# Attention values of 512 queries in every fourth slot, with the softmax sums applied after the product

## The chip, the cores and the metric

The kernel runs on one core of a Trainium2 chip. The metric is the device time of one execution in microseconds. The names of the engines are those of the profile: PE (TensorE, with PEld for its weight loads), DVE (VectorE), ACT (ScalarE), POOL (GpSimd) and SP (SyncE, which issues nearly all transfers of the kernel before).

## The reference

All data are float32. A graph-attention layer comes first, and then a transformer block whose attention is the part that matters here. It has four batches of 1024 rows, 16 heads of 64 columns, and nothing is masked:

```
qkv  = modulate(layernorm(x)) @ W_qkv          # x: 4 x 1024 x 512
attn = softmax(q @ k.T * 64**-0.5)             # per batch and head: 1024 x 1024
out  = attn @ v                                # 4 x 1024 x (16 heads x 64)
x    = x + g_msa * (out @ W_out + b_out)
x    = x + g_mlp * (gelu(modulate(layernorm(x)) @ W1 + b1) @ W2 + b2)
```

## The kernel before

The graph layer runs up to about 410 us of the span. The attention stage follows, to about 2226 us, and then the MLP.

The attention stage is cut into `NS` = 256 **slots**: four batches, eight pairs of heads (`gp`), eight tiles `t` of 128 queries. Slot `s` makes the scores of its 128 queries against all 1024 keys for both heads of the pair (`scores`, L1156: four matmuls in the program, eight records in the profile), into two PSUM tiles `psc` of two banks each, of which there are two, so that a slot's scores wait until both exponentials of the slot before have read them. VectorE takes the two maxima (`largest`, L1167), ScalarE makes the two exponentials with their sums (`weights`, L1173). `scaled` (L1178 to L1182) inverts each sum on VectorE and multiplies the 128x1024 weights by it, for head 0 on ScalarE (L1180), for head 1 on GpSimd (L1182). `turn` (L1191) transposes the weights on VectorE in blocks of 32x32 into `wd`; it is called for the slot before, head 0 at the beginning of a slot, head 1 after the two maxima.

Two successive slots make a **unit** `k` of 256 queries. When the second of them is transposed, eight copies of 256 KB (four for each head, L1195) issued by SP carry `wd` into `wT`, where the keys stand on the partitions. `wd` has three buffers, each for one head of one unit; `wT` has two, each for a whole unit. `attend` (L1064) multiplies a unit's `wT` with the values: 16 matmuls of 256 columns in the program, 32 records in the profile. ScalarE copies the product from PSUM to `oT` (L1076).

The rest of the work is laid between as fill: the projections of q, k and v for later heads in a form with seven products instead of eight (`seven`, L533, with VectorE's corrections in L547 and L551), the output projection in the same form (`out_step`, L1139), whose products VectorE adds to the rows `xr` (L1148), and sums of weights on GpSimd (L504 to L512). A planner places the fill: every item has a first and a last slot, a weight in units of TensorE's time, and a place within the slot. It looks for the slots in which the sum of the squares of the loads is small, with a price on two value products in one slot. `LAG` = 4 sets the distance from a unit's first slot to its `attend`:

```
lo = at + QT * k + LAG
add(lo, lo + (lo < NS - 8), 2, 1, attend, b, gp, k)
```

Within an engine the instructions run in the order in which the program gives them. Tiles are rotated within their pool: a tile that takes over a buffer waits for the last use of the one before it, on whichever engine that is.

```
wd[j] = ap_.tile([P, 4 * KC, QT, U], F32, name="wd", tag="wd", bufs=3)
wT[b, gp, k] = ap_.tile([P, 2, 4, KC, QT * U], F32, name="wT", tag="wT", bufs=2)
```

Of the kernel before, what the change touches and what calls it, by code (L numbers as in the profile page):

```python
# [41 lines left out]
def cond_block_kernel(  # L42
# [898 lines left out]
    with ExitStack() as actx:  # L941
# [9 lines left out]
        NB = S // QB  # L951
        wout, gate = {}, {}
        vt, oT, xr, wn, wd, wT = {}, {}, {}, {}, {}, {}

        turns = []

# [98 lines left out]
        def attend(b, gp, k, a=0, z=KC):  # L1055

            if a == 0:
                pav[0] = ps.tile([P, F], F32, name="pav", tag="pav")[:, :QB]
            po = pav[0]
            g, p = divmod(gp, 2)  # L1060
            w = wT[b, gp, k]
            for m in range(a, z):
                for j in range(2):
                    nc.tensor.matmul(  # L1064
                        po[j * D : (j + 1) * D, :],
                        lhsT=vt[b, g][:, m, p * P + j * D : p * P + (j + 1) * D],
                        rhs=w[:, j, :, m, :],
                        start=(m == 0),
                        stop=(m == KC - 1),
                    )  # L1070
# [53 lines left out]
        def out_step(b, g, u, k):  # L1124
            which, fresh, (i, j) = PU[k]
            if fresh:
                pu[0] = ps.tile([P, F], F32, name="pu", tag="pu")
            if which in SUM_A:
                a = osum[b, g][:, SUM_A[which] * HB : (SUM_A[which] + 1) * HB]
            else:  # L1130
                h, f = {0: (0, 0), 1: (0, 1), 3: (1, 1), 6: (1, 0)}[which]
                a = oT[b, 2 * g + f, u][:, h * QB : (h + 1) * QB]
            if which in SUM_B:
                r = wsum[b, g][:, SUM_B[which] * HB : (SUM_B[which] + 1) * HB]
            else:
                f, h = {0: (0, 0), 1: (1, 0), 2: (1, 1), 6: (0, 1)}[which]
                r = wout[b, g][:, f, h * HB : (h + 1) * HB]
            for q in range(2):
                nc.tensor.matmul(  # L1139
                    pu[0][:, q * HB : (q + 1) * HB],  # L1140
                    lhsT=a[:, q * P : (q + 1) * P],
                    rhs=r,
                    start=(bool(fresh) and q == 0),
                    stop=True,
                    skip_group_check=True,
                )
            o = xr[b, 2 * u + i][:, :, j * HB : (j + 1) * HB]
            nc.vector.tensor_tensor(o, pu[0].rearrange("p (r f) -> p r f", r=2), o, ALU.add)  # L1148


        def scores(b, gp, t):
# [15 lines left out]
            nc.vector.tensor_reduce(mx, sc, axis=AX.X, op=ALU.max, negate=True)  # L1167
            return mx

        def weights(sc, mx):  # L1170
            w = ap_.tile([P, S], F32, name="w", tag="w", bufs=4)
            sm = ap_.tile([P, 1], F32, name="sm", tag="sm", bufs=4)
            nc.scalar.activation(w, sc, AF.Exp, bias=mx, accum_out=sm)  # L1173
            return w, sm

        def scaled(j, w, sm):

            nc.vector.reciprocal(sm, sm)  # L1178
            if j == 0:
                nc.scalar.mul(w, w, sm)  # L1180
            else:
                nc.gpsimd.tensor_scalar(w, w, sm, None, ALU.mult)  # L1182

        def turn(b, gp, t, j):

# [54 lines left out]
        for b in range(B):  # L1240
# [252 lines left out]

        row_sum(0, 2)
        emit(-3, 0)
        before = None
        for s in range(NS + 1):
            if before is not None:
                turn(*before[0], 0)
            while later:  # L1500
                later.pop(0)()
            if s < NS:
                b, r = divmod(s, NP * NT)
                gp, t = divmod(r, NT)
                sc = scores(b, gp, t)
                mx = [largest(sc[j]) for j in range(2)]
                early(s)
                ws = [weights(sc[j], mx[j]) for j in range(2)]
                now = ((b, gp, t), ws)
                scaled(0, *ws[0])  # L1510
            if before is not None:
                turn(*before[0], 1)
            before = None
            if s < NS:
                scaled(1, *ws[1])
                for j in range(2):
                    wn[(*now[0], j)] = ws[j][0]
                before = now
            if s < NS:
                emit(s, s + 1)  # L1520
        sc_banks = halves()
        late = []
        second = with_four(
# [199 lines left out]
```

## Time and profile before

| | |
|---|---|
| time, median of 3 runs | 3037.48 us (3035.5 to 3040.55) |
| span of the profiled execution | 3034.2 us; the median lies 3.3 us above it |
| busy: PE, DVE, ACT, POOL | 99%, 66%, 47%, 44% |
| copies wT<-wd | 1024 of 256 KB |
| TensorE's granted clock | 1.00 in every stretch looked at |

The profile is of one execution. A row of the page's groups gives the line, the engine, the operation, what it writes and reads, how often, the busy time and the mean length of one, and then the engine's idle time just before and who ended it. In the chain and in the timeline the first number is the start in us, the second the length. SPq stands for SP's queue of transfers. TensorE runs each float32 matmul as two records.

### The profile page before, as it was taken

To read this page: it belongs to the slowest core of one execution; us is meant where nothing else is said; L and a number is where in the kernel's file an instruction comes from. 1 tells how busy PE (TensorE), PEld (TensorE's weight loads), DVE (VectorE), ACT (ScalarE), POOL (GpSimd) and SP (SyncE) were. 2 spreads that over 40 slices of the span, in tenths; PEclk is the share of its full clock that TensorE was granted. 3 is DMA by queue.
4 is the path that set the end of the run, shared out by engine and by line. 5 is a ranking of instruction groups with operands and counts; after the bars stand their busy time and mean duration, and the time that the engine had idled before them with its cause. 6 is when DMAs were issued, how large, how long until landed. Compare 5 with 4: busy or idle time off the path is not lost.

```text
span 3034.2 us, 41780 instructions
## 1 busy us (share of the span) xinstructions
PE 2999.3 (99%) x15317; PEld 1980.2 (65%) x15317; DVE 1999.6 (66%) x2836; ACT 1432.0 (47%) x2368; POOL 1339.4 (44%) x922
## 2 busy tenths in 40 slices
PE   9999999999999999999999999999999999999999
PEld 6666655555555555555555555555568888888888
DVE  3888867777878877878787878877863222222322
ACT  3344456555755565755555755556641221112211
POOL 1444456555656655656655656655721110111010
PEclk9999999999999999999999999999999999999999
DMA  6433357777868777768777868766871010101110
GB/s 201 140 118 121 117 129 180 162 171 179 192 157 210 181 168 179 192 155 211 187 159 180 191 159 205 189 162 164 203 196 63 14 49 28 49 21 35 35 42 15
DMA packets 282695, 417.90 MB, mean 138 GB/s; under 512 B 28968, under 2 KB 101092, under 8 KB 282492
## 3 DMA queue, kind: packets, MB, share of 16 engines
q1 hardware_dynamic: 282256, 415.03, 53.8%
q8 instruction: 123, 2.02, 0.3%
q14 instruction: 80, 0.66, 0.1%
q10 hardware_dynamic: 236, 0.20, 0.0%
HBM read 120.93 MB, written 25.76 MB: 48 GB/s over the span
## 4 chain that ended last, share of the span: by engine, by line
PE 83%; DVE 7%; ACT 3%; POOL 3%; issue 2%; DMA 2%; SPq 1%; POOLq 0%; DVEq 0%; ACTq 0%
PE q L533 19%; PE psc L1156 15%; PE pav L1064 13%; PE pu L1139 6%; PE mbd L533 5%; PE mbu L533 5%; PE mad L533 4%; PE mau L533 3%; PE mcd L533 2%; PE mdd L533 2%; PE mdu L533 2%; PE mcu L533 2%; DVE mx L1167 1%; ACT w L1173 1%; POOL t L742 1%
## 5 line engine op out<-in xcount | busy, mean ns | idle before, releaser
L1182 POOL TENSOR_SCALAR w<-w,sm 128x1024 f32<-128x1024 f32 x256 | 728.6, 2846 | 701.5 <-DVE sm L1178 686.4
L1173 ACT ACTIVATE w<-psc,mx 128x1024 f32<-128x1024 f32 x512 | 570.7, 1115 | 642.6 <-DVE mx L1167 641.6
L1191 DVE STREAM_TRANSPOSE wd<-w 128x1024 f32<-128x1024 f32 x512 | 632.2, 1235 | 109.3 <-ACT w L1180 96.0
L1167 DVE TENSOR_REDUCE mx<-psc 128x1 f32<-128x1024 f32 x512 | 599.2, 1211 | 80.2 <-PE psc L1156 77.0
L1156 PE MATMUL psc<-kT,qT 64*128 64x512 f32 x2048 | 526.9, 615 | 3.1 <-ACT kT L1024 1.4
L1064 PE MATMUL pav<-wT,v 128*64 128x256 f32 x4096 | 482.1, 383 | 1.2 <-DMA wT<-wd 0.6
L1064 PEld LDWEIGHTS pav<-wT,v 128*64 128x64 f32 x4096 | 296.1, 137 | 224.0 <-issue 86.0
L1156 PEld LDWEIGHTS psc<-kT,qT 64*128 64x128 f32 x2048 | 201.6, 186 | 220.5 <-issue 151.2
L1180 ACT ACTIVATE w<-w,sm 128x1024 f32<-128x1024 f32 x256 | 291.0, 1137 | 0.0
L512 POOL TENSOR_TENSOR tx<-hT 128x512 f32<-128x512 f32 x8 | 10.3, 1288 | 596.5 <-ACT hT L448 596.5
L1148 DVE TENSOR_TENSOR xr<-pu,xr 128x512 f32<-128x512 f32 x210 | 143.5, 683 | 78.9 <-PE pu L1139 78.7
L533 PE MATMUL q<-hT,wqk 128*128 128x512 f32 (+1 forms) x396 | 181.2, 581 | 1.0 <-DVE q L547 1.0
L555 ACT COPY mbu<-mau 128x512 f32<-128x512 f32 x30 | 17.1, 570 | 276.5 <-PE mau L533 276.5
L719 PE MATMUL pa<-kp,sfT 128*128 128x320 f32 x512 | 143.5, 433 | 1.4 <-ACT sfT L694 1.4
L533 PEld LDWEIGHTS q<-hT,wqk 128*128 128x128 f32 x396 | 74.7, 190 | 80.9 <-issue 78.2
L533 PE MATMUL q<-tx,ex 128*128 128x512 f32 (+1 forms) x264 | 123.5, 591 | 1.8 <-POOL tx L618 1.3
L719 PEld LDWEIGHTS pa<-kp,sfT 128*128 128x128 f32 x512 | 94.8, 190 | 38.2 <-ACT sfT L694 1.9
L679 PE MATMUL pf<-wx,xT 128*128 128x512 f32 x256 | 116.0, 596 | 0.0
L533 PE MATMUL mad<-w,hs 128*128 128x256 f32 x512 | 113.1, 379 | 0.0
L533 PEld LDWEIGHTS mad<-w,hs 128*128 128x128 f32 x512 | 97.3, 190 | 13.2
L1139 PE MATMUL pu<-wout,oT 128*128 128x256 f32 x360 | 98.4, 396 | 4.2 <-DVE xr L1148 3.7
L1139 PEld LDWEIGHTS pu<-wout,oT 128*128 128x128 f32 x360 | 62.6, 189 | 59.3 <-issue 31.6
(309 smaller groups left out, 4590.7 us busy)
## 6 DMA issues: line engine op xcount, KB each, us to landing
wT<-wd SPq DMA_DIRECT2D x1024, 256.0 KB
wqk<-in_w_qkv SPq DMA_DIRECT2D x64, 256.0 KB
xT<-in_xt SPq DMA_DIRECT2D x32, 256.0 KB
xs<-in_x SPq DMA_DIRECT2D x32, 256.0 KB
x1d<-xs SPq DMA_DIRECT2D x32, 256.0 KB
xl<-x1d SPq DMA_DIRECT2D x32, 256.0 KB
wv<-in_w_qkv SPq DMA_DIRECT2D x32, 256.0 KB
xr<-x1d SPq DMA_DIRECT2D x32, 256.0 KB
```

What stands on the lines that cost most here:

```text
L533: nc.tensor.matmul(t[:, q * width : (q + 1) * width], lhsT=lhs(which, q, k), rhs=rhs(which, q, k), start=(fresh and q == 0 and k == 0), st ...
L679: nc.tensor.matmul(pfs[i], lhsT=xT[i][:, c, :], rhs=wx[:, c, :], start=False, stop=(c == FC - 1), skip_group_check=True,)
L719: nc.tensor.matmul(pas[i][:, n, :HF], lhsT=sfT2[i][:, c, :], rhs=kp[:, b, c, n * HF : (n + 1) * HF], start=False, stop=(c == FC - 1), skip ...
L1064: nc.tensor.matmul(po[j * D : (j + 1) * D, :], lhsT=vt[b, g][:, m, p * P + j * D : p * P + (j + 1) * D], rhs=w[:, j, :, m, :], start=(m == 0),
L1139: nc.tensor.matmul(pu[0][:, q * HB : (q + 1) * HB], lhsT=a[:, q * P : (q + 1) * P], rhs=r, start=(bool(fresh) and q == 0), stop=True, skip ...
L1148: nc.vector.tensor_tensor(o, pu[0].rearrange("p (r f) -> p r f", r=2), o, ALU.add)
L1156: nc.tensor.matmul(sc[j][:, n * F : (n + 1) * F], lhsT=qT[b, gp][q, t * P : (t + 1) * P], rhs=kT[b, gp][q, n * F : (n + 1) * F], start=Tru ...
L1167: nc.vector.tensor_reduce(mx, sc, axis=AX.X, op=ALU.max, negate=True)
L1173: nc.scalar.activation(w, sc, AF.Exp, bias=mx, accum_out=sm)
L1180: nc.scalar.mul(w, w, sm)
L1182: nc.gpsimd.tensor_scalar(w, w, sm, None, ALU.mult)
L1191: nc.vector.transpose(wd[j][:, :, at, :], wn.pop((b, gp, t, j)).rearrange("p (m k) -> p m k", k=U))
```

## The change

The weights are no longer scaled. The exponentials leave their sums in one small tile per unit (`sm`, 128x4, in `weights`); when a unit's second slot is done, `scales_out` inverts the four columns on VectorE, and a slot later a DMA issued by ScalarE writes them to a small DRAM tile `scd`; two slots after the unit `scales_in` reads them back with two more DMAs of ScalarE's, spread over 64 partitions for each head (`rB`). VectorE multiplies the value product in PSUM with `rB` on its way to `oT`, in place of ScalarE's copy.

`turn` is called for the slot's own weights, both heads after the exponentials, instead of for those of the slot before. The weights `w` have two buffers instead of four.

Where a pair of heads is not among the last two, `attend_two` replaces two calls of `attend`: the value products of units 2u and 2u+1 follow each other into one PSUM bank, as one item of weight 4, with the first slot at the second unit's place.

The products of the output projection leave PSUM by a copy of ScalarE's into `po` (two buffers), and GpSimd adds them to `xr`.

```diff
+    scd = [tc.dram_tile([4, P], F32, name=f"scd{i}") for i in range(4)]
...
-            nc.scalar.copy(
+            nc.vector.tensor_tensor(
                 oT[b, gp, u][:, i * QB : (i + 1) * QB].rearrange("p (t u q) -> p u t q", t=QT, u=4),
                 po.rearrange("p (u t q) -> p u t q", t=QT, u=4),
+                rB.pop((b, gp, k)).rearrange("p (t u q) -> p u t q", t=QT, u=4),
+                ALU.mult,
             )
+        def attend_two(b, gp, u):
+            po = ps.tile([P, F], F32, name="pav", tag="pav")
+            g, p = divmod(gp, 2)
+            for k in (2 * u, 2 * u + 1):
+                w = wT[b, gp, k]
+                for m in range(KC):
+                    for j in range(2):
+                        nc.tensor.matmul(
+                            po[j * D : (j + 1) * D, k % 2 * QB : (k % 2 + 1) * QB],
+                            lhsT=vt[b, g][:, m, p * P + j * D : p * P + (j + 1) * D],
+                            rhs=w[:, j, :, m, :],
...
+            t = op_.tile([P, F], F32, name="oT", tag="oT", bufs=6)
+            oT[b, gp, u] = t
+            for k in range(2):
+                cols = slice(k * QB, (k + 1) * QB)
+                nc.vector.tensor_tensor(
...
-            nc.vector.tensor_tensor(o, pu[0].rearrange("p (r f) -> p r f", r=2), o, ALU.add)
+            t = ap_.tile([P, F], F32, name="po", tag="po", bufs=2)
+            nc.scalar.copy(t, pu[0])
+            nc.gpsimd.tensor_tensor(o, t.rearrange("p (r f) -> p r f", r=2), o, ALU.add)
...
-            w = ap_.tile([P, S], F32, name="w", tag="w", bufs=4)
-            sm = ap_.tile([P, 1], F32, name="sm", tag="sm", bufs=4)
-            nc.scalar.activation(w, sc, AF.Exp, bias=mx, accum_out=sm)
+            w = ap_.tile([P, S], F32, name="w", tag="w", bufs=2)
+            if (b, gp, k) not in esum:
+                esum[b, gp, k] = ap_.tile([P, 2 * QT], F32, name="sm", tag="sm", bufs=2)
+            c = j * QT + at
+            nc.scalar.activation(w, sc, AF.Exp, bias=mx, accum_out=esum[b, gp, k][:, c : c + 1])
...
+        def scales_out(b, gp, k):
+            sm = esum.pop((b, gp, k))
             nc.vector.reciprocal(sm, sm)
-            if j == 0:
-                nc.scalar.mul(w, w, sm)
-            else:
-                nc.gpsimd.tensor_scalar(w, w, sm, None, ALU.mult)
+            spot[0] += 1
+            scales[b, gp, k] = scd[spot[0] % len(scd)]
+            return lambda: nc.scalar.dma_start(scales[b, gp, k].rearrange("c p -> p c"), sm)
+        def scales_in(b, gp, k):
...
+                nc.scalar.dma_start(
+                    rB[b, gp, k][j * D : (j + 1) * D, :],
+                    row(rows[j * QT : (j + 1) * QT, :].rearrange("t q -> (t q)")).broadcast_to([D, QB]),
+                )
...
-                for k in range(NB):
+                if at < NS - 2 * NT:
+                    for u in range(NB // 2):
+                        lo = at + QT * (2 * u + 1) + LAG
+                        add(lo, lo + 1, 4, 1, attend_two, b, gp, u)
+                for k in range(NB if at >= NS - 2 * NT else 0):
                     lo = at + QT * k + LAG
...
+            sc = scores(b, gp, t)
+            mx = [largest(sc[j]) for j in range(2)]
+            early(s)
+            for j in range(2):
+                weights(b, gp, t, j, sc[j], mx[j])
+            for j in range(2):
+                turn(b, gp, t, j)
+            while coming and coming[0][0] <= s:
+                coming.pop(0)[1]()
+            if t % QT == QT - 1:
+                key = b, gp, t // QT
+                coming.append((s + 1, scales_out(*key)))
+                coming.append((s + 2, lambda key=key: scales_in(*key)))
+            emit(s, s + 1)
```

In the changed file the maxima are L1199, the exponentials L1208, the reciprocals L1214, the DMAs of the sums L1217 and L1224, the transposes L1236, the copies L1240, the double value product L1093 with the multiplications L1104, and the output products' copy and addition L1179 and L1180. Slot numbers below count within a pair of heads, from its first slot; unit k has the slots 2k and 2k+1, and where the text speaks of slot X, it is 4u+6, the first in which the double product of units 2u and 2u+1 may stand.

More of the change, by code (lines that the diff above doesn't have):

```diff
@@ L953, in cond_block_kernel @@
         vt, oT, xr, wn, wd, wT = {}, {}, {}, {}, {}, {}
+        esum, scales, rB, spot = {}, {}, {}, [0]
         turns = []
@@ L1075, in attend @@
                 oT[b, gp, u] = op_.tile([P, F], F32, name="oT", tag="oT", bufs=6)
-            nc.scalar.copy(
+            nc.vector.tensor_tensor(
                 oT[b, gp, u][:, i * QB : (i + 1) * QB].rearrange("p (t u q) -> p u t q", t=QT, u=4),
                 po.rearrange("p (u t q) -> p u t q", t=QT, u=4),
-            )
+                rB.pop((b, gp, k)).rearrange("p (t u q) -> p u t q", t=QT, u=4),
+                ALU.mult,
+            )
+        def attend_two(b, gp, u):
[9 more added lines that the diff above has]
+                            rhs=w[:, j, :, m, :],
+                            start=(m == 0),
+                            stop=(m == KC - 1),
+                        )
[4 more added lines that the diff above has]
+                nc.vector.tensor_tensor(
+                    t[:, cols].rearrange("p (t u q) -> p u t q", t=QT, u=4),
+                    po[:, cols].rearrange("p (u t q) -> p u t q", t=QT, u=4),
+                    rB.pop((b, gp, 2 * u + k)).rearrange("p (t u q) -> p u t q", t=QT, u=4),
+                    ALU.mult,
+                )
         def project(b, g, n):
@@ L1168, in largest, with weights @@
             return mx
-        def weights(sc, mx):
-            w = ap_.tile([P, S], F32, name="w", tag="w", bufs=4)
-            sm = ap_.tile([P, 1], F32, name="sm", tag="sm", bufs=4)
[L1173 to L1178, printed above, removed]
-            if j == 0:
-                nc.scalar.mul(w, w, sm)
-            else:
-                nc.gpsimd.tensor_scalar(w, w, sm, None, ALU.mult)
+        def weights(b, gp, t, j, sc, mx):
+            k, at = divmod(t, QT)
+            w = ap_.tile([P, S], F32, name="w", tag="w", bufs=2)
[3 more added lines that the diff above has]
+            nc.scalar.activation(w, sc, AF.Exp, bias=mx, accum_out=esum[b, gp, k][:, c : c + 1])
+            wn[b, gp, t, j] = w
+        def scales_out(b, gp, k):
+            sm = esum.pop((b, gp, k))
+            nc.vector.reciprocal(sm, sm)
+            spot[0] += 1
+            scales[b, gp, k] = scd[spot[0] % len(scd)]
+            return lambda: nc.scalar.dma_start(scales[b, gp, k].rearrange("c p -> p c"), sm)
+        def scales_in(b, gp, k):
+            rows = scales.pop((b, gp, k))
+            rB[b, gp, k] = ap_.tile([P, QB], F32, name="rB", tag="rB", bufs=4)
+            for j in range(2):
+                nc.scalar.dma_start(
+                    rB[b, gp, k][j * D : (j + 1) * D, :],
+                    row(rows[j * QT : (j + 1) * QT, :].rearrange("t q -> (t q)")).broadcast_to([D, QB]),
+                )
         def turn(b, gp, t, j):
@@ L1495, in cond_block_kernel @@
         emit(-3, 0)
[L1496 to L1499, printed above, removed]
+        coming = []
+        for s in range(NS):
             while later:
                 later.pop(0)()
[L1502 to L1520, printed above, removed]
+            b, r = divmod(s, NP * NT)
+            gp, t = divmod(r, NT)
+            sc = scores(b, gp, t)
[3 more added lines that the diff above has]
+                weights(b, gp, t, j, sc[j], mx[j])
+            for j in range(2):
+                turn(b, gp, t, j)
[6 more added lines that the diff above has]
+            emit(s, s + 1)
+        while later:
+            later.pop(0)()
+        for _, f in coming:
+            f()
         sc_banks = halves()
```

## The prediction

> **What bounds the kernel now.** I read the page first, for who is busy and what its chain runs through; then the chain in one stretch of the attention stage, for the length of a slot's pieces; then one slot in order of time, for the latencies between engines; last who waits for the transposed weights, because the change touches their buffers' timing.
>
> ```profile
> PE 2999.3 (99%) x15317; PEld 1980.2 (65%) x15317; DVE 1999.6 (66%) x2836; ACT 1432.0 (47%) x2368; POOL 1339.4 (44%) x922
> ...
> PE q L533 19%; PE psc L1156 15%; PE pav L1064 13%; PE pu L1139 6%; PE mbd L533 5%; PE mbu L533 5%; PE mad L533 4%; PE mau L533 3%; PE mcd L533 2%; PE mdd L533 2%; PE mdu L533 2%; PE mcu L533 2%; DVE mx L1167 1%; ACT w L1173 1%; POOL t L742 1%
> ...
> L1182 POOL TENSOR_SCALAR w<-w,sm 128x1024 f32<-128x1024 f32 x256 | 728.6, 2846 | 701.5 <-DVE sm L1178 686.4
> L1173 ACT ACTIVATE w<-psc,mx 128x1024 f32<-128x1024 f32 x512 | 570.7, 1115 | 642.6 <-DVE mx L1167 641.6
> L1191 DVE STREAM_TRANSPOSE wd<-w 128x1024 f32<-128x1024 f32 x512 | 632.2, 1235 | 109.3 <-ACT w L1180 96.0
> L1167 DVE TENSOR_REDUCE mx<-psc 128x1 f32<-128x1024 f32 x512 | 599.2, 1211 | 80.2 <-PE psc L1156 77.0
> ...
> L1180 ACT ACTIVATE w<-w,sm 128x1024 f32<-128x1024 f32 x256 | 291.0, 1137 | 0.0
> ```
>
> TensorE is always busy, and the chain hardly leaves it. The two scalings of the weights (L1180, L1182), which the change removes, cost 1020 us, but ScalarE and GpSimd each sit idle some 640 to 700 us beside them: none of it is on the chain. The chain between 1000 and 1300 us gives the pieces of a slot:
>
> ```profile
> 1000.26 1.92 PE psc L1156 x8
> 1002.18 3.60 PE pav L1064 x32
> 1005.79 3.63 PE q L533 x8
> 1009.42 1.92 PE psc L1156 x8
> ```
>
> Scores are 1.92 us a slot; a value group of 256 queries is 3.60, in every second slot; the rest is projections. One slot in order of time (start, length):
>
> ```profile
> 1300.82 8.73 SPq L1195 DMA_DIRECT2D wT<-wd  x8
> ...
> 1301.10 3.67 PE L1064 MATMUL pav<-wT,v 128*64 128x256 f32 x32
> 1301.56 2.33 DVE L1167 TENSOR_REDUCE mx<-psc 128x1 f32<-128x1024 f32 x2
> ...
> 1302.79 1.11 ACT L1173 ACTIVATE w<-psc,mx 128x1024 f32<-128x1024 f32 x1 [2.83 <-DVE mx L1167]
> 1303.80 0.19 ACT L1173 ACTIVATION_READ_ACCUMULATOR w<-psc,mx 128x1 f32 x1
> ...
> 1303.98 1.12 ACT L1173 ACTIVATE w<-psc,mx 128x1024 f32<-128x1024 f32 x1
> ```
>
> From the first maximum's start to the end of the first exponential with its sum are 2.4 us, to the end of the second 3.5. The view of tile wd says what VectorE's transposes wait for:
>
> ```profile
> its engine sat idle before it (us, times) until:
>   ACT w L1180: 96.0, 119
>   DMA wT<-wd: 3.9, 6
> ```
>
> Before the change a transpose almost never waits for the copies that empty its buffer. That is the line to remember. The stage's 256 slots run from 408.5 us (first score matmul) to about 2226: 7.10 us a slot, 28.4 a period of four.
>
> **What the change removes and adds.** ScalarE loses 256 scalings (291 us) and 128 copies of 0.36 us, and gains 210 copies of 0.57 (120 us) and 384 DMA issues; GpSimd loses 728.6 us and gains 210 additions of 1.27 us (row L984, 128x512), 267 us; VectorE loses 210 additions of 0.683 and 512 reciprocals of 0.14, and gains 128 multiplications and 128 reciprocals. A multiplication (128x256, one operand in PSUM) is not in the trace: half of L1148 is 0.34 us, half of L551, which writes scattered elements, 0.52; it is nearer the first: 0.4. An issue from ScalarE has no row in this stage; SyncE's own take 0.54 to 2.53 us, median 0.97, for far larger copies. I take 0.6: 1.5 a slot, behind the exponentials, where 1.14 us of scaling went. At 2.5 us they would fill ScalarE; that is left to the upper case. All of this is cover that nobody waited for, so it is priced at nothing. TensorE's matmuls stay the same in number. Counted over the changed program's order with the spacing of records in the trace (1.92 scores, 3.60 a value group, 0.43 a record of 512 columns, 0.216 of 256, 0.112 of 128), four slots hold 27.5 us on average (21.8 to 30.4). So of today's 28.4 at most 0.9 us a period can be won, some 57 us over the stage.
>
> **What it moves, and the wait it makes.** Transposes now stand in their own slot, so unit k (two slots, 256 queries) sends its copies wd to wT in slot 2k+1, a slot earlier than before. The value product of units 2u and 2u+1 stands in slot X = 4u+6, both halves. But wT has two buffers and wd three. The copies of unit 2u+2, issued in slot X-1, write the buffer that unit 2u holds until the first half of X is through: they stand at the head of SyncE's queue until then, and loads behind them too. And VectorE's second transpose in slot X (head 1 of unit 2u+3) needs the wd buffer that head 0 of unit 2u+2 has not yet emptied. The changed program's order shows both waits: that transpose waits for four copies, whose first waits for the sixteenth value matmul of the same slot. Queued behind that transpose on VectorE are the two multiplications and both maxima of the next slot; ScalarE's exponentials wait for those, and the scores two slots on for the exponentials.
>
> How long do four copies take? From the trace's semaphore updates: first issue to the landing of the fourth, 7.7 us median over 101 groups (7.2 to 8.3 for nine in ten), idle rings or not. A single copy has 4.75.
>
> The cycle from slot X's scores to slot X+4's, each step waiting for the one before:
> - scores 1.92, first half 3.60, release 0.1: 5.6
> - four copies of unit 2u+2: 7.7, so the transpose starts at 13.3 instead of about 5.5
> - transpose 1.24 and two multiplications 0.8: 15.4, where slot X+1's maxima start
> - to the end of the first exponential with its sum, and the semaphore: 2.6; transpose of head 0: 1.24, which frees the copies of unit 2u+3: 19.2
> - four copies again, 7.8 with the release: the second transpose of slot X+2 (unit 2u+4) needs their buffer: starts at 27.0. In the old order 1.6 slots, 11 us, lay between these two; now less than one
> - transpose 1.24, the correction of q (L547) 0.69: 28.9, maxima of slot X+3
> - second exponential's end 3.5: 32.4, and scores of X+4 can go.
>
> TensorE's own path is shorter: it is through with X+1's 6.2 us at 15.3, waits for X+1's second exponential until 18.9 (15.4 + 3.5), and has 27.5 + 3.6 = 31.1 us in a period. So the cycle sets it: 32.4 against 28.4, 4.0 us in each of 60 periods, 240 us; the last 16 slots keep the single groups. On the profiled execution's span: 3034.2 + 240 = 3274; the median of the runs shown lies 3.3 above the span: **3278 us**. With the smallest of each row (four copies 7.2, no L547, multiplications at 0.34) the cycle is 30.5, 126 us; with the largest (8.3, L547, 1.04 for L551 too, multiplications at 0.52) 34.8, 384 us.
>
> The Trainium skill has a rule that would turn the sign. "DMA: Bandwidth & Descriptors", in the section on the anatomy of one DMA, fits 2.0 us plus the bytes over 436 GB/s; four copies of 256 KB would by that (an estimate) take 4.4 us together. Then the second wait is gone, the first costs TensorE 0.3 us a period, and the kernel gains some 40 us. The trace's 7.7 us decides against it.
>
> **Rivals.**
> - *Only the first wait counts* (chance 0.15): the copies of unit 2u+3 find empty rings and land inside slot X+2. Then TensorE's path of 31.1 us holds: 2.7 a period, 162 us, 3200. Against it: that asks for 5.5 us or so, and no group of four was under 7.
> - *More is held up* (0.15): SyncE's queue stands still 6 us in each period with weight loads behind it, GpSimd's sums wait for these, ScalarE's PSUM copies wait for GpSimd's additions through two buffers (po), and ScalarE's exponentials stand behind its own issues. One more such wait of 1.5 us a period is 90 us: 3368. For it: the old chain has stretches that run through wout's and xl's loads.
> - *Faster* (0.04): VectorE's wait is covered, since TensorE has the second half (3.6) and X+1's work (6.2) to do meanwhile. That holds from the point where the four copies land within 4.2 us (15.3 - 3.5 - 2.0 - 5.6). Then the stage is TensorE's 27.5 a period: 3037.5 - 57 = 2980. Against it the 7.7, nearly double.
> - *No change* (0.01): wins and waits would have to cancel.
>
> **How the numbers follow.** The two waits as worked out have 0.65, by their own bounds 3164 to 3421, most of it 3210 to 3350. Two runs of this kernel can be told apart from 0.2% on, 6 us. Faster 0.04, the same 0.01, slower 0.95. The range takes in the lower bound of the cycle and the first rival below, and above it the second rival with half of what the cycle's upper bound adds: 3155 to 3390.
>
> **What would show it.** Right: in the changed profile VectorE's transpose L1236 waits for the DMA wT<-wd some 5 us in every fourth slot, and a lesser time two slots on (hundreds of us in all, 3.9 now); TensorE's busy share falls in the stage, its scores waiting for the exponentials; GpSimd and ScalarE idle. Slots come in fours of about 32 us, none longer than the rest for want of POOL. Wrong: if that wait is small or TensorE still 99% busy, the cycle is not there; if the transposes wait as said but the period is well off 32, the landing time or a step behind it was mis-sized; if ScalarE's idle time ends on POOL, or L1224's issues are microseconds long, the second rival had it.

## The result and the profile after

The changed kernel takes **3552.7 us** (median of four, 3544.7 to 3557.3), the kernel before beside it 3039.0: a ratio of 1.168 [1.166, 1.171]. The forecast was 3278, in a range of 3155 to 3390. The side was right; the loss is 514 us instead of 240.

The page of the changed kernel, in the order of the lines shown of before:

```profile
PE 3237.0 (91%) x15317; PEld 2076.3 (59%) x15317; DVE 1885.4 (53%) x2370; ACT 1236.5 (35%) x2194; POOL 876.9 (25%) x876
...
PEclk9999989899998889898988989889899999999999
...
PE 57%; DMA 14%; SPq 8%; DVE 4%; ACT 2%; issue 2%; ACTq 0%; POOL 0%; DVEq 0%; POOLq 0%
...
L1236 DVE STREAM_TRANSPOSE wd<-w 128x1024 f32<-128x1024 f32 x512 | 621.9, 1235 | 791.9 <-DMA wT<-wd 690.8
L1188 PE MATMUL psc<-kT,qT 64*128 64x512 f32 x2048 | 690.9, 706 | 240.4 <-ACT w L1208 238.1
L1208 ACT ACTIVATE w<-psc,mx 128x1024 f32<-128x1024 f32 x512 | 570.2, 1115 | 890.1 <-DVE mx L1199 889.4
```

Three things are new. VectorE's transposes now stand idle behind the copies wT<-wd, as forecast: 690.8 us. TensorE's scores wait for exponentials, those for maxima, and the maxima stand behind the transposes. And PEclk is no longer at 1.00: TensorE's 15317 instructions are as many as before, but take 3237 us instead of 2999. The view of tile wd:

```profile
its engine sat idle before it (us, times) until:
  DMA wT<-wd: 690.8, 116
  ACT w L1208: 78.2, 201
```

3.9 us in 6 waits have become 690.8 in 116, nearly two in each of the 60 periods counted in the prediction. One period in the timeline of the changed kernel (start, length, and in brackets the idle time before, with who ended it):

```profile
1294.91 0.37 ACTq L1217 DMA_DIRECT2D scd<-sm  x1
...
1296.28 8.52 SPq L1240 DMA_DIRECT2D wT<-wd  x8
...
1305.77 1.25 DVE L1236 STREAM_TRANSPOSE wd<-w 128x1024 f32<-128x1024 f32 x1 [8.98 <-DMA wT<-wd]
1306.94 0.72 DVE L1104 TENSOR_TENSOR oT<-pav,rB 128x256 f32<-128x256 f32 x2
1307.58 2.34 DVE L1199 TENSOR_REDUCE mx<-psc 128x1 f32<-128x1024 f32 x2
1308.88 1.11 ACT L1208 ACTIVATE w<-psc,mx 128x1024 f32<-128x1024 f32 x1 [12.28 <-DVE mx L1199]
...
1310.14 4.91 PE L1188 MATMUL psc<-kT,qT 64*128 64x512 f32 x8 [4.03 <-ACT w L1208]
...
1319.57 1.25 DVE L1236 STREAM_TRANSPOSE wd<-w 128x1024 f32<-128x1024 f32 x1 [1.81 <-DMA wT<-wd]
```

The cycle of the prediction is there, step by step: copies, transpose, multiplications, maxima, exponential, scores. But the first copies are 9.4 us on their way (1296.28 to the transpose, less a tenth), not 7.7, with the new store of the sums going out 1.4 us ahead of them. And the scores take 4.91 us instead of 1.99. Why shows in the view by windows (us, busy time and count of PE, PEld, DVE, ACT, POOL, then PEclk, DMA share, GB/s):

```profile
1298.00:1308.00 10.00, 8.11 (x36) 3.75 (x32) 2.23 (x4) 0.00 (x0) 0.00 (x0) 1.00 0.97 225
...
1310.00:1320.00 10.00, 9.86 (x18) 4.86 (x19) 7.06 (x8) 5.12 (x10) 2.54 (x2) 0.57 0.70 156
1320.00:1330.00 10.00, 10.00 (x40) 4.75 (x40) 7.68 (x9) 4.84 (x8) 5.37 (x6) 1.00 0.47 82
```

Around TensorE's wait of 4.03 us its granted clock is halved, here for 10.24 us. The trace's clock record holds 59 such stretches between the graph layer and the end of the kernel, nearly as many as there are periods: 30 of 6.83 us, 18 of 10.24, and the others between 3.41 and 13.65. The kernel before has none there. They go with TensorE's idle gaps: none of 33 gaps of 0.3 to 1 us has one, 2 of 14 between 1 and 2 us do, 10 of 13 between 2 and 3, and all 46 above 3.

The medians over all periods of the stage, each step by itself, from the same records (us; their sum need not be the median period):

| step of the cycle | predicted | measured |
|---|---|---|
| scores and first half of the product | 5.6 | 5.6 |
| four copies, first issue to fourth landing | 7.7 | 9.5 |
| transpose | 1.24 | 1.24 |
| two multiplications | 0.8 | 0.56 |
| maxima's start to the next transpose's end | 3.84 | 3.8 |
| four copies again | 7.7 | 7.95 |
| second transpose and what lies ahead of slot X+3's maxima | 1.9 | 2.9 |
| from there to the second exponential's end | 3.5 | 3.6 |
| from there to the scores of slot X+4 | 0 | 0.7 |
| the period | 32.4 | 36.4 |

In the means, with the short waits between them, the steps do add up to the period of 36.4. Of the 4.0 us above the forecast 1.8 lie in the first four copies, 0.4 in the second four, 0.9 ahead of slot X+3's maxima, and 0.4 between the second exponential and the scores; what is left is small.

From the start of the first scores to the start of the last ones the stage takes 2307 us (1814 before): 493 more, and what follows 826.5 instead of 811.5: 15 more. That is the 508 us between the spans.

### The profile page after: what moved, and what is told of

It is laid out like the page before. It is cut to its first block, busy times and chain, and to the rows that moved or that the text cites. A ratio compares the mean times of both kernels' runs of the same rounds, so it can differ in the third digit from the quotient of the medians.

```text
span 3542.2 us, 42053 instructions
## 1 busy us (share of the span) xinstructions
PE 3237.0 (91%) x15317; PEld 2076.3 (59%) x15317; DVE 1885.4 (53%) x2370; ACT 1236.5 (35%) x2194; POOL 876.9 (25%) x876
## 4 chain that ended last, share of the span: by engine, by line
PE 57%; DMA 14%; SPq 8%; DVE 4%; ACT 2%; issue 2%; ACTq 0%; POOL 0%; DVEq 0%; POOLq 0%
PE psc L1188 13%; PE q L534 10%; DMA wT<-wd 10%; SPq L1240 7%; PE pav L1093 6%; PE mbd L534 5%; PE pu L1169 4%; PE mbu L534 4%; PE mad L534 3%; PE mau L534 3%; DMA scd<-sm 2%; ACT w L1208 2%; DVE mx L1199 2%; PE mcd L534 2%; PE mdd L534 2%
## 5 line engine op out<-in xcount | busy, mean ns | idle before, releaser
L1236 DVE STREAM_TRANSPOSE wd<-w 128x1024 f32<-128x1024 f32 x512 | 621.9, 1235 | 791.9 <-DMA wT<-wd 690.8
L1188 PE MATMUL psc<-kT,qT 64*128 64x512 f32 x2048 | 690.9, 706 | 240.4 <-ACT w L1208 238.1
L1208 ACT ACTIVATE w<-psc,mx 128x1024 f32<-128x1024 f32 x512 | 570.2, 1115 | 890.1 <-DVE mx L1199 889.4
L1199 DVE TENSOR_REDUCE mx<-psc 128x1 f32<-128x1024 f32 x512 | 602.5, 1214 | 129.7 <-PE psc L1188 129.3
L1180 POOL TENSOR_TENSOR xr<-po,xr 128x512 f32<-128x512 f32 x210 | 266.8, 1271 | 1449.7 <-ACT po L1179 1396.4
L1188 PEld LDWEIGHTS psc<-kT,qT 64*128 64x128 f32 x2048 | 246.7, 208 | 550.1 <-ACT w L1208 341.0
L1093 PE MATMUL pav<-wT,v 128*64 128x256 f32 x3840 | 427.6, 381 | 0.0
L1093 PEld LDWEIGHTS pav<-wT,v 128*64 128x64 f32 x3840 | 270.5, 137 | 175.4 <-issue 30.3
L1179 ACT COPY po<-pu 128x512 f32<-128x512 f32 x210 | 122.9, 585 | 251.9 <-PE pu L1169 143.7
L534 PE MATMUL q<-hT,wqk 128*128 128x512 f32 (+1 forms) x396 | 192.3, 611 | 9.9 <-DVE q L548 4.7
L534 PE MATMUL q<-tx,ex 128*128 128x512 f32 (+1 forms) x264 | 143.2, 672 | 2.4 <-ACT v L1047 2.4
L1169 PE MATMUL pu<-wout,oT 128*128 128x256 f32 x360 | 120.6, 465 | 2.7 <-ACT po L1179 2.7
L1208 ACT ACTIVATION_READ_ACCUMULATOR w<-psc,mx 128x1 f32 x512 | 99.8, 195 | 0.0
```

Of the source, the lines that this page charges most:

```text
L534: nc.tensor.matmul(t[:, q * width : (q + 1) * width], lhsT=lhs(which, q, k), rhs=rhs(which, q, k), start=(fresh and q == 0 and k == 0), st ...
L1093: nc.tensor.matmul(po[j * D : (j + 1) * D, k % 2 * QB : (k % 2 + 1) * QB], lhsT=vt[b, g][:, m, p * P + j * D : p * P + (j + 1) * D], rhs=w ...
L1169: nc.tensor.matmul(pu[0][:, q * HB : (q + 1) * HB], lhsT=a[:, q * P : (q + 1) * P], rhs=r, start=(bool(fresh) and q == 0), stop=True, skip ...
L1179: nc.scalar.copy(t, pu[0])
L1180: nc.gpsimd.tensor_tensor(o, t.rearrange("p (r f) -> p r f", r=2), o, ALU.add)
L1188: nc.tensor.matmul(sc[j][:, n * F : (n + 1) * F], lhsT=qT[b, gp][q, t * P : (t + 1) * P], rhs=kT[b, gp][q, n * F : (n + 1) * F], start=Tru ...
```

## The experiments

The theory on record had the cycle of blocked copies; "the block" below is the wait of unit 2u+2's copies until the first half of slot X's product has read the buffer. Its rivals after the result: the transfers of the sums, which the prediction had priced at nothing; the clock, which it had not priced; and the detour of the output products. Every ratio below is to the kernel before, run beside it.

### Is it the double product?

**single** keeps everything else but multiplies single value groups; **two_only** is the kernel before with the double product alone.

```diff
# single
-                if at < NS - 2 * NT:
+                if False:
...
-                for k in range(NB if at >= NS - 2 * NT else 0):
+                for k in range(NB):
# two_only: the kernel before with attend_two, its products copied by ScalarE, and the same items in the planner
```

> The changed kernel, but with one value group of 256 queries in every second slot, as before the change; all else of the change stays (unscaled weights, sums through DRAM, transposes in their own slot, output products by ScalarE and GpSimd). Theory (the double group holds back the copies of unit 2u+2, and with them VectorE): the copies find their wT buffer free, the long waits of the transposes for wT<-wd go, no drop of TensorE's clock; a wait of 0 to 1 us stays where the second transpose of a unit's first slot needs the buffer of the unit before. 3040 us, between 3000 and 3120. Rival (the sums' DMAs, ScalarE's issues or the new way out of PSUM cost the time): over 3400, with the waits still there.

> The kernel before, with the double value group in every fourth slot and nothing else of the change: weights scaled, transposes a slot late, products copied by ScalarE. Theory: the copies of unit 2u+2 are issued at the beginning of slot X and blocked until its first half is through, but the transpose that needs their buffer stands in slot X+1, after its maxima, some 13 us after slot X's start, when they land: little is lost, 3020 to 3130 us, no drop of the clock. The long wait needs both the double group and the transposes in their own slot. Rival (the double group alone makes the wait): 3300 us or more, with VectorE waiting for wT<-wd some 5 us in every fourth slot.

Measured: two_only 3071.8, 1.010 [1.008, 1.012], as expected. single 3289.3, 1.082 [1.079, 1.085]: missed by 250 us. The double product is harmless in the old order of transposes, and taking it out of the changed kernel returns only half of the loss. So something else costs some 250 us, and not through the cycle. In single, ScalarE's waits show it:

```profile
ACT w L1208 <- DVE mx L1199: 301.4, 126, 7.9
ACT po L1179 <- issue: 284.7, 63, 8.6
```

ScalarE's copies of output products wait 284.7 us for "issue", nothing that the profile can name, up to 8.6 us at a time. It stands at its own transfers: in 61 of the 63 waits the two loads of the sums are what stands in ScalarE's order just ahead of the copy. And the loads wait for the store that writes what they read. One store and its first load in the timeline of single:

```profile
1256.47 0.37 ACTq L1217 DMA_DIRECT2D scd<-sm  x1
...
1265.37 2.30 ACTq L1224 DMA_DIRECT2D rB<-scd  x2
```

By the trace's semaphore updates 119 of single's 128 pairs of loads are issued within 0.4 us of the landing of their store, 9.7 us after its issue in the median. ScalarE had come to 114 of them earlier, by 300 us in all. In the changed kernel, whose slots are longer, this holds for 46 pairs, and ScalarE stood some 58 us before them.

### Is it the block of the copies alone?

**lag3** puts the double product a slot earlier, so that wT comes free before the next copies need it.

```diff
-                        lo = at + QT * (2 * u + 1) + LAG
+                        lo = at + QT * (2 * u + 1) + LAG - 1
```

> The changed kernel with the double group one slot earlier (LAG - 1: slots 5, 9, 13 and so on instead of 6, 10, 14). Theory: the first half ends at 5.6 us of the slot, before the slot's first transpose is done (5.4 to 6.7), so the copies of unit 2u+2 are never blocked; instead TensorE may wait up to 1 to 2 us for the copies of unit 2u+1, issued two slots earlier. 3010 to 3130 us. Rival (the double group as such, 7.2 us of TensorE in one slot, starves the other engines): within 100 us of the changed kernel's 3550.

Measured: 3473.7, 1.143 [1.138, 1.149]: missed. **nosums** leaves the transfers of the sums out and multiplies by a constant; **nosums_single** and **nosums_lag3** join that with the two edits above. In all three the softmax's normalisation is left out.

```diff
-            return lambda: nc.scalar.dma_start(scales[b, gp, k].rearrange("c p -> p c"), sm)
+            return lambda: None
...   # and in scales_in, instead of the two loads:
+            if "one" not in rB:
+                rB["one"] = ap_.tile([P, QB], F32, name="rB", tag="rB", bufs=1)
+                nc.vector.memset(rB["one"], 1.0 / S)
+            rB[b, gp, k] = rB["one"]
```

> The changed kernel without the three DMAs of each unit's inverse sums; the products are multiplied by one constant tile instead, so the normalisation is left out. In the changed kernel's trace the four copies of head 0 take 9.5 us from issue to landing after the block, not 7.7, and the store of the sums (512 elements of 4 bytes, 8.8 us to land) is issued just before them. Theory: that store slows the copies; without it they land in 7.7 us again, 1.8 us a period less, some 110 us: 3440 us, the waits and the clock's drops stay. Rival (the copies are slow for another reason, or the store is hidden): 3530 to 3560. Second rival (the sums' DMAs are the cause of the whole loss): below 3150.

> The kernel with single value groups (single) and without the sums' DMAs (normalisation left out). Theory: of single's 250 us nearly all come from these DMAs: the store of 4-byte elements takes 8.8 us to land, ScalarE's next issue waits for it with exponentials and copies behind it, the copies wT<-wd share the engines with it, and the stage's end waits for it once more (15 us). Without them and without the double group there is no wait left: 3000 to 3050 us. Rival (transposes in the slot of their own weights, with wd's three buffers, cost the 250 us): 3200 or more, with transposes waiting for wT<-wd over 150 us in all.

> The double group one slot earlier (lag3) without the sums' DMAs (normalisation left out). Theory: copies of unit 2u+2 are never blocked, those of unit 2u+1 land 12.5 us after the first transposes of two slots before, about when the second half wants them: TensorE waits 1 to 2 us a period at most, 3020 to 3130 us. Against nosums (3390) this takes away the block alone, with the double group kept. Rival (the double group starves the other engines, blocked copies or not): above 3300.

Measured: nosums 3389.9, 1.114 [1.112, 1.117], 163 us less than the changed kernel, more than expected; the four copies land in 7.85 us again, the period is 34.5. nosums_single 3064.6, 1.008 [1.006, 1.010], 15 above its range; nosums_lag3 3093.8, 1.019 [1.017, 1.020]. With the sums' transfers out of the way the block of the copies can be weighed alone, the slow clock behind it included: one slot's shift of the double product takes 3390 to 3094, **296 us**. The 55 us that nosums_lag3 still lies above the kernel before were not parted (two_only lies 32 above it, out_only 10). Its waits confirm it; VectorE's transposes in nosums, then in nosums_lag3:

```profile
DVE wd L1234 <- DMA wT<-wd: 627.1, 120, 13.1
```

```profile
DVE wd L1234 <- DMA wT<-wd: 141.6, 62, 7.9
```

So both are shown: the block, which the prediction had, and the sums' transfers, worth 163 us where the block stands and 225 (3289 to 3065) or 380 (3474 to 3094) where it does not.

### What does the clock cost?

**warm** fills TensorE's wait in the changed kernel with four matmuls that add zeros, at the end of slot X+1; **nosums_warm** does so with three in nosums.

```diff
             emit(s, s + 1)
+            if s % 4 == 3 and s < NS - 2 * NT:
+                for _ in range(4):
+                    nc.tensor.matmul(q2, lhsT=zero, rhs=gates, start=False, stop=True, skip_group_check=True)
```

> The changed kernel with four more matmuls of 512 columns (3.4 us) at the end of each slot X+1 before slot 240; their stationary operand is zero and they add to the bank q2 of the projections, so nothing changes in the result. In the changed kernel's trace TensorE stands idle some 4.9 us there, the granted clock drops to 0.5 for some 10 us after it in 60 places, and the period of four slots is 36.4 us. Theory (the drop is the second part that the prediction had not priced; the waits of VectorE set the rest): the idle time shrinks to 1.5 us, the clock stays at 1.0, and the period falls to VectorE's own cycle, 34.4 us: 2.0 x 60, 120 us less, 3430 us, in spite of 206 us of added matmuls. Rival (the slow clock lies beside waits that are there anyway, and the added work costs time): 3540 us or more.

> The kernel without the sums' DMAs (nosums, normalisation left out) with three such added matmuls of zeros in each slot X+1. Period of nosums: 34.5 us at 3390 us. Theory: with neither the slow copies nor the slow clock the period is the cycle that the prediction summed, 32.4 us; 3270 us. Rival: no gain, 3390 or more.

Measured: warm 3659.2, 1.204 [1.201, 1.206]: slower by 106 us instead of faster. Its first four copies landed later still (10.7 us; why was not tried), so that 3.5 us of idle time a period (4.3 in the changed kernel) and 47 of the low stretches remained. It says nothing of the clock. nosums_warm can be read: 3326.2, 1.095 [1.093, 1.096], above the 3270 expected but 64 us less than nosums although 155 us of matmuls came on top (60 periods of 6 records of 0.43). The windows from 450 to 2500 us of nosums, then of nosums_warm, PEclk third from the end:

```profile
450.00:2500.00 2050.00, 1874.80 (x9165) 1028.90 (x9161) 1253.53 (x1332) 827.27 (x1425) 597.96 (x624) 0.93 0.63 148
```

```profile
450.00:2500.00 2050.00, 1979.66 (x9890) 1074.07 (x9892) 1301.82 (x1386) 865.93 (x1493) 632.55 (x660) 0.99 0.65 155
```

More work in a stalled engine made the kernel faster, since the work after the stall then ran at the full clock: 7 low stretches are left of 43 in the stage. The expectations' "some 10 us" for such a stretch is too long for most, as said above. The period falls from 34.5 to 33.0, near the 32.4 of the prediction, which had reckoned with a full clock.

### What of the sums' transfers costs?

The store writes 512 elements of 4 bytes. By the packet records its last packet ends some 3.6 us after the issue (median), but it lands only after 8.8 us (nine in ten from 7.6 to 9.9). **wide**, **single_wide** and **lag3_wide** let VectorE turn the tile of sums in 32x32 blocks and store runs of 128 bytes. **single_store** keeps the store as it is and leaves the loads out; its product is multiplied by a constant.

```diff
+            sT = ap_.tile([P, U], F32, name="sT", tag="sT", bufs=2)
+            nc.vector.transpose(sT, sm)          # sm is 128x32 here, four columns of it used
...
-            return lambda: nc.scalar.dma_start(scales[b, gp, k].rearrange("c p -> p c"), sm)
+            def store():
+                for a in range(P // U):
+                    nc.scalar.dma_start(scales[b, gp, k][:, a * U : (a + 1) * U], sT[a * U : a * U + 2 * QT, :])
+            return store
```

> The changed kernel with the inverse sums stored in runs of 128 bytes: VectorE turns the tile of sums in blocks of 32, and four transfers of 4 rows by 128 bytes leave, instead of one of 512 elements of 4 bytes. Theory A, the small elements hold up the copies that share the rings: copies land near 7.9 us again (9.55 in the changed kernel, 7.85 without the sums' transfers), a period falls from 36.4 to 34.5 to 35, 3553 becomes 3390 to 3450. Rival B, it is the round trip itself (order of issue on ScalarE, waits for landings): within 30 us of 3553.

> The changed kernel with single value groups (3289) and the sums stored in runs of 128 bytes. Theory A, small elements: most of the 225 us between it and the same kernel without the sums' transfers (3065) comes back: 3070 to 3130. Rival B, the round trip itself: 3250 to 3320.

> The changed kernel with the double value group one slot earlier (3474) and the sums stored in runs of 128 bytes. Theory A, small elements: near 3094, what it is without the sums' transfers: 3095 to 3170. Rival B, the round trip itself: 3430 to 3510.

> Single value groups (3289) with the store of the inverse sums in its 4-byte elements kept and their loads left out; the output products are multiplied by a constant, so the normalisation is left out. Theory A, the store's elements: most of the 225 us stays, 3200 to 3290. Rival B, the loads and the wait for the store's landing ahead of them: 3065 to 3120.

Measured: wide 3492.4, 1.150 [1.147, 1.153]; single_wide 3172.6, 1.044 [1.042, 1.046]; lag3_wide 3220.2, 1.061 [1.058, 1.063]; single_store 3206.8, 1.055 [1.053, 1.057]. Only the last fell where theory A had it; the first three lie between the theories. In wide the first four copies land in 7.79 us again (9.5 in the changed kernel): the copies' extra 1.7 us are due to the small elements. The page counts packets under 512 bytes, in the changed kernel and then in wide:

```profile
DMA packets 370760, 434.97 MB, mean 123 GB/s; under 512 B 100648, under 2 KB 189156, under 8 KB 370556
```

```profile
DMA packets 307276, 435.01 MB, mean 124 GB/s; under 512 B 37160, under 2 KB 125668, under 8 KB 307068
```

Nearly the same bytes, and 63488 packets under 512 bytes fewer. The Trainium skill, "DMA: Bandwidth & Descriptors", asks in its table of specifications for transfers of at least 512 bytes and says that smaller ones are read, modified and written. Runs of 128 bytes are small by that too; the runs show only that they no longer hold up the copies.

But the period of wide is still 36.2 in the median (36.0 in the mean, 36.4 in the changed kernel). Its second half is longer, and ScalarE's waits name the store:

```profile
ACT po L1180 <- DMA scd<-sT: 126.4, 29, 6.8
```

The changed kernel's program shows how that comes. The transfers of SP and ScalarE take the same semaphores in turn, and an issue waits until the transfer that used its semaphore before has landed. So 339 of ScalarE's 384 transfers follow a copy of wT on their semaphore, and 314 of SP's 1024 copies a transfer of the sums. Most find it free: in the changed kernel's trace 33 of the 339 and 45 of the 314 are issued within 0.1 us of the landing before them, as an issue is that had to wait. In wide 208 of the 285 stores that follow a copy are. Behind an issue of ScalarE's stand, in order, its PSUM copies and exponentials. wide issues four stores for one, which makes more such pairs: its 60 us are what the longer runs save less what these cost. The other side, SP's copies waiting for the sums, in the changed kernel's waits:

```profile
SPq L1240 <- DMA scd<-sm: 42.3, 36, 4.6
```

### Do the two queues hold each other up?

A first try moved the loads one slot later (**single_wide_late**, **wide_late**), when the store has long landed. The second issued store and loads from GpSimd (**single_wide_pool**, **wide_pool**), whose transfers in the program wait for no copy, nor any copy for them.

```diff
# late
-                coming.append((s + 2, lambda key=key: scales_in(*key)))
+                coming.append((s + 3, lambda key=key: scales_in(*key)))
# pool, for the store and both loads
-nc.scalar.dma_start(
+nc.gpsimd.dma_start(
```

> Single value groups, sums stored in runs of 128 bytes (3173), and their loads issued one slot later, when the store has landed. Theory A, what is left of the sums' cost is ScalarE held in order by the wait for the store's landing: 3070 to 3110, near the 3065 without the sums' transfers. Rival B, the transfers themselves: 3150 to 3190.

> The changed kernel with the sums stored in runs of 128 bytes (3492) and their loads issued one slot later. Theory A, ScalarE held by the wait for the store's landing: 3390 to 3420, near the 3390 without the sums' transfers. Rival B, the transfers themselves: 3470 to 3500.

> Single value groups, sums stored in runs of 128 bytes (3173), store and loads issued by GpSimd instead of ScalarE. Theory A, ScalarE held at its issues until earlier copies land is what is left: 3065 to 3100. Rival B, the transfers themselves: 3150 or more.

> The changed kernel with the sums stored in runs of 128 bytes (3492), store and loads issued by GpSimd. Theory A, ScalarE held at its issues: 3385 to 3425, near the 3390 without the sums' transfers. Rival B, the transfers themselves: 3470 or more.

Measured: single_wide_late 3432.1, 1.129 [1.127, 1.131], and wide_late 3673.5, 1.209 [1.207, 1.211]: 260 and 181 us slower than without the move, outside both theories. The edit made a queue of its own: the loads now stand just ahead of the next unit's store, six issues in a row. ScalarE's waits and, last, VectorE's in single_wide_late:

```profile
ACT po L1180 <- DMA scd<-sT: 156.3, 23, 8.9
ACT v L1048 <- DMA scd<-sT: 122.8, 18, 9.1
ACT kT L1027 <- DMA scd<-sT: 119.3, 22, 10.2
ACT qT L1025 <- DMA scd<-sT: 88.7, 15, 7.6
```

```profile
DVE oT L1079 <- DMA rB<-scd: 257.2, 100, 5.1
```

ScalarE is held 487 us in these four rows (166 in single_wide), and the multiplications now wait for the loads. The theory had named ScalarE's wait for the store's landing. That held for single, but with runs of 128 bytes little of it was left to win: in single_wide 50 of 128 pairs of loads are issued within 0.4 us of their store's landing, and ScalarE stood only some 17 us before them. What costs here is the place in the order of the two queues.

single_wide_pool 3059.8, 1.007 [1.005, 1.008], and wide_pool 3379.6, 1.112 [1.110, 1.114]: 5 us below theory A's ranges, and below the kernels without these transfers (3065 and 3390). In neither does a wait of ScalarE's end on a transfer of scd, rB or wT any more. So the sums' 173 us (3553 to 3380) go in two steps: 60 with the longer runs, net of the added issues, and 113 with the move to GpSimd. These are not the shares of the changed kernel, since wide has waits at its four stores that the changed kernel has not. How much of the 113 is ScalarE's waits, how much SP's and how much the length of the issues on ScalarE was not parted.

### And the output products?

**out_only** is the kernel before with their detour alone (w with three buffers, for room); **dveadd** is the changed kernel without it.

```diff
# dveadd; out_only is the reverse, in the kernel before
-            t = ap_.tile([P, F], F32, name="po", tag="po", bufs=2)
-            nc.scalar.copy(t, pu[0])
-            nc.gpsimd.tensor_tensor(o, t.rearrange("p (r f) -> p r f", r=2), o, ALU.add)
+            nc.vector.tensor_tensor(o, pu[0].rearrange("p (r f) -> p r f", r=2), o, ALU.add)
```

> The kernel before with only this part of the change: output products copied from PSUM by ScalarE and added by GpSimd (exp's tile w has three buffers instead of four, for room). Theory, priced at nothing: 3020 to 3060. Rival, the detour carries a good part of the loss (ScalarE's queue holds the exps back): 3100 or more.

> The changed kernel (3553) with only this part undone: VectorE adds the output products from PSUM as before. Theory, priced at nothing: 3530 to 3580. Rival, the detour over ScalarE carries a good part of the loss: 3500 or less.

Measured: out_only 3049.4, 1.0033 [1.0022, 1.0043], a loss of 10 us. dveadd 3648.2, 1.200 [1.198, 1.202]: undoing this part costs 95 us, outside both expectations. TensorE's wait in dveadd says why it isn't worth nothing there:

```profile
PE pu L1169 <- DVE xr L1178: 147.1, 50, 9.4
```

With VectorE blocked up to 17 us at its transposes, the product's PSUM bank is not emptied; the changed kernel waits 7.9 us for its copies on ScalarE. The detour saves what the block would have cost. The first four copies also land later in dveadd (11.0 us); why was not tried.

No version that computes the whole reference ran faster than the kernel before. The nearest are out_only (3049) and single_wide_pool (3060).

## Why the prediction was wrong in size

**The block was right.** The two waits, their place, the queue behind them and their two per period are in the trace as forecast, and nosums_lag3 shows that they carry 296 us. The fit of the page, by which four copies would land in 4.4 us and the change gain 40, does not hold for these copies: the first four of a period took 7.65 to 7.9 us in every kernel with the block and without 4-byte stores. The page gives the fit for transfers issued by GpSimd, and these are SP's. The rivals "only the first wait counts" and "faster" fell with it. The rival "more is held up" named ScalarE's exponentials behind its own issues, which came true, but as a small rival of 90 us; and GpSimd, whose additions it named too, held ScalarE's copies up for only some 26 us (17.0, 6.6 and 2.3 in ScalarE's waits).

**The failed step was "all of this is cover that nobody waited for, so it is priced at nothing".** It counted ScalarE's 384 issues by their length (0.6 us; measured 0.37 for a store, 0.46 for a load) and left out what an issue waits for and what the transfers do to others. They cost 163 us by nosums, 173 by wide_pool against the changed kernel. In the changed kernel most of that is the store's effect on the copies: its mean period is 2.0 us longer than that of nosums (36.4, 34.4), and 1.7 of these lie in the first four copies, some 100 us in 60 periods (an estimate from these means). 14 lie behind the stage: with the transfers, the work after the start of the last scores takes 826.5 us, in wide_pool 812.3. ScalarE's order, behind the store's landing and behind copies on the same semaphores, weighs more where the block is gone: in single the transfers cost 225 us, and ScalarE stands 300 us before its loads.

**The term "four copies: 7.7 us" was mis-sized** for the same reason. It was read off the old program, where no 4-byte store goes ahead of the copies: 9.5 with it, 7.79 in wide.

**The clock was left out.** The prediction worked out itself that TensorE would wait 3.6 us in each period, and then went on with durations at full clock. Scores of slot X+2 took 4.91 us. nosums_warm puts this at 64 us or more, since the gain is net of 155 us of added matmuls. The Trainium skill, "TensorE: Matmul & The Clock Gate", in its part on the clock gate, lets an idle window of about 3.4 us halve the clock and 3.4 us of work restore it. The trace agrees on the half, but has it after 56 of 59 gaps above 2 us, and for 6.83 us or more in 53 of 59 stretches.

The miss of 274 us (3553 against 3278) then adds up: 173 for the sums' transfers, 64 for the clock (3390 to 3326), and 36 for the 0.6 us by which nosums_warm's period of 33.0 exceeds 32.4, 60 times. This mixes runs of different kernels, and the parts are not strictly additive: the sums cost 163, 225 or 380 us by what else stands in the way.

The range has a slip of its own. By the rule that the prediction gives for its upper end, the second rival with half of what the cycle's upper bound adds, it is 3368 + 72 = 3440, not 3390. The measured time lies above both.

## What to carry to other kernels

A DMA issue costs its engine not its own half microsecond but the time until its semaphore is free and its source is ready. On an engine that others wait for in order, look in the program at what every new issue waits for, or issue from an engine that nobody waits for. Where an estimate makes TensorE wait 2 us or more per period, add the slow clock behind the wait to the sum. And durations of copies hold only beside the traffic in which they were measured; a store of single elements changes them.

## What the runs showed of the hardware

- A store of 2 KB in elements of 4 bytes took 8.8 us to land and delayed the four 256 KB copies issued behind it by 1.7 us (9.5 against 7.79 with runs of 128 bytes).
- TensorE's clock fell to a half around every one of 46 waits above 3 us, for 3.4 to 13.7 us and most often 6.8, so that a stalled engine given 155 us of useless work let the kernel finish 64 us sooner.
- Transfers on two queues can hold each other up with no data between them, through the semaphores that they share: in wide 208 of 285 stores were issued within 0.1 us of the landing of the copy that had used their semaphore before.
